# Layer 0 of a two-layer attention and FFN kernel: the order of second maxima on the vector engine, and one square root more on the scalar engine

## Chip, cores, metric

The kernel runs on one core of one Trainium2 chip. The metric is the device time of one execution in microseconds (us), as the median of several runs. Times inside an execution come from one execution taken by the hardware profiler. The engines are called PE (matrix), DVE (vector), ACT (scalar), POOL (GpSimd) and SP (the queue that issues the DMAs); each works through its own queue in order and waits for the others by semaphores.

## What is computed

Two layers over x (32 sequences of 64 tokens, width 512), all in 32-bit floats. Only layer 0 matters here: a cross attention, and an FFN in which every block of 32 hidden units keeps the one with the largest score.

```python
def _L0_xattn_ref(text, features, Wq_w, Wq_b, Wk_w, Wk_b, fn_w, qn_w, kn_w):
    features_n = rmsnorm(features, fn_w)
    Q = jnp.einsum('btd,fd->btf', text, Wq_w) + Wq_b
    K = jnp.einsum('bsd,fd->bsf', features_n, Wk_w) + Wk_b
    Q = rmsnorm(Q, qn_w)
    K = rmsnorm(K, kn_w)
    scores = jnp.einsum('btf,bsf->bts', Q, K) * scale
    attn = jax.nn.softmax(scores, axis=-1)
    return jnp.einsum('bts,bsf->btf', attn, features_n)

def _L0_ffn_ref(x, c1_w, c2_w, w1, w2t):      # INTER 1792, SPARSITY 32
    xf = x.reshape(B * T, M)
    inter = xf @ c1_w.T @ c2_w.T
    blk = inter.reshape(B * T, n_blocks, SPARSITY)
    idx = jnp.argmax(blk, axis=-1) + jnp.arange(0, INTER, SPARSITY)
    h = jax.nn.relu(jnp.einsum('bkm,bm->bk', w1[idx], xf))
    return jnp.einsum('bk,bkm->bm', h, w2t[idx]).reshape(B, T, M)

x = x + _L0_xattn_ref(_layernorm(x), ctx_4096, ...)
x = x + _L0_ffn_ref(_layernorm(x), ...)
x = x + _L1_xattn_ref(_layernorm(x), ctx_4096, ...)
x = x + _L1_ffn_ref(_layernorm(x), ...)
```

## The kernel before

The tokens lie in 16 tiles of 128, and layer 0's attention runs over them in eight groups of two tiles (`i` = 0 to 7, "pairs"). The work of neighbouring pairs is interleaved: while the keys and queries of pair `i` are made, the scores of pair `i - 1` and the values of pair `i - 2` are finished. In one round PE does, in this order: `pt` (the normed tokens turned, L181), `pk` (keys, sixteen products of 128x512, L372), `pa_t` (the softmaxed scores turned, L454), `ptk` (the keys turned), `po` (values, L466), `psc` (scores, L427), and `pq` (queries, sixteen products, L392), `ptq` (the queries turned). The other engines take the results out of PSUM. DVE adds the bias to the keys (`kb`, L375) and to the queries (`qb`, L393), scales keys by their norm (`kb`, L410), copies turned keys with a weight (`kT`, L415), and adds the values to x (L472). ACT squares rows for the norms (`scr`, L379 and L395), takes the square roots (`sq`, L354), copies `xT`, `qT` and `aT`, and takes the exponentials (`s`, L440).

The FFN's argmax for the first two pairs of tokens is computed ahead, between these steps. `PLAN` gives for (pair, place) what is put there; place 0 is ahead of the keys, 1 behind the scores, 2 behind the queries. For a group `p` of 256 tokens, `two_quarters(p, v)` makes the scores of two quarters (448 hidden units, `pi`, L277) of 128 tokens, four times per group, so that a group has eight quarters. `first_largest` finds the position of the largest score of each block of 32 in four steps: DVE takes the maximum `m` (L267) and compares (`e`, L268, which is also the last reader of the PSUM bank), POOL multiplies the comparison by a ramp that falls with the position (`e`, L272), and DVE takes the maximum again (`choice`, L273). The last step is returned as a function; `two_quarters` puts it into the list `begun`, and `choose_begun` runs whatever the list holds at the start of the next `two_quarters`, or in `turn_choice`, which turns the finished choices of a group and writes them to memory.

`pk`, `pq`, `pi` and `po` share three PSUM banks in turn (`ps_m`). So the first `pk` behind two pairs of quarters needs the bank of the fourth comparison.

POOL has other work in this stage: sums of pieces of W1 and W2 for a Strassen-Winograd scheme (`four_sums`, L127). For W2 a piece is loaded (`w2p`, one buffer), summed, stored (`w2s`), and then the next is loaded. All loads and stores stand in SP's queue, which they share with the loads of context (`ct`, `cn`) for the pair after the next.

The order on each engine is settled when the kernel is built: a list scheduler takes the instructions as they are traced, moves them by priority, and respects data, buffers and the extra edges that `tc.issue_after(ins)` adds. Such an edge puts what is traced in the block behind `ins` where both run on one engine. 

ACT holds one function table at a time; a square root behind an exponential, or the reverse, needs a load first (ACT_TABLE_LOAD). The square and the copies load none. For the last pair `queries_of` ends with an exponential of zero times `sq` into `one` (L404), behind the roots, so that the table is there when the last scores come; `scores` multiplies by `one` (L436).

Of the kernel before, what the change touches and what calls it, by code (L numbers as in the profile page):

```python
# [8 lines left out]
F32 = mybir.dt.float32  # L9
I32 = mybir.dt.int32  # L10
BF16 = mybir.dt.bfloat16
AF = mybir.ActivationFunctionType
# [4 lines left out]
P = 128  # L17
# [6 lines left out]
QW = 448  # L24
# [11 lines left out]
def tile_kernel(  # L36
# [25 lines left out]
    nc = tc.nc  # L62
# [11 lines left out]
    eps6 = const.tile([P, 1], F32, name="eps6")  # L74
# [104 lines left out]
    def transposed(ps, src):  # L179
        for c in range(C):  # L180
            nc.tensor.transpose(ps[:, c, :], src[:, c * P : (c + 1) * P], ident)  # L181


    with ExitStack() as l0:
# [74 lines left out]
        def first_largest(pi, e, choice, n):  # L259


            w, k = n * QW, n * NBQ
            mx = small.tile([P, k], F32, name=f"m{n}", tag=f"m{n}", bufs=2)
            e4 = e.rearrange("p (n a b) -> p n a b", n=n, b=BLK)
            pi = pi.rearrange("p n (a b) -> p n a b", b=BLK)
            mx3 = mx.rearrange("p (n a) -> p n a", n=n)
            nc.vector.tensor_reduce(mx3, pi, AX.X, ALU.max)  # L267
            nc.vector.tensor_tensor(  # L268
                e4, pi, mx3[:, :, :, None].to_broadcast([P, n, NBQ, BLK]), ALU.is_equal
            )  # L270
            e3 = e.rearrange("p (a b) -> p a b", b=BLK)
            nc.gpsimd.tensor_tensor(e3, e3, down[:, None, :].to_broadcast([P, k, BLK]), ALU.mult)  # L272
            return lambda: nc.vector.tensor_reduce(choice, e3, AX.X, ALU.max)  # L273

        def key_product(out, z, m, q):
            rows = slice(32 * q, 32 * q + RANK)
            nc.tensor.matmul(out, z[rows, m * P : (m + 1) * P], C2R[rows, :], start=True, stop=True)  # L277
# [10 lines left out]
        def new_choices():  # L288
            return [prepool.tile([P, 4 * NBQ], F32, name="choice", tag="choice", bufs=2) for _ in range(2)]

        with ExitStack() as pa:
            wpool = pa.enter_context(tc.tile_pool(name="l0w", bufs=1))
            wk = pa.enter_context(tc.tile_pool(name="l0work", bufs=2))
# [6 lines left out]
            bq = wpool.tile([P, D], F32, name="bq")  # L300
# [4 lines left out]
            one = wpool.tile([P, 1], F32, name="one")  # L305
# [47 lines left out]
            def norm_of(sq):  # L353
                nc.scalar.activation(sq, sq, AF.Sqrt, bias=eps6, scale=1.0 / D)  # L354
                nc.vector.reciprocal(sq, sq)
# [26 lines left out]
            def queries_of(i, xT, sq, between):  # L382

                qT = wk.tile([P, 2, C, P], F32, name=f"qT_{i}", tag="qT")
                qb = wk.tile([P, 2, D], F32, name="qb", tag="qb", bufs=1)
                last = i == NP - 1
                if last:
                    norm_of(sq[:, 2:4])
                for tt in range(2):
                    pq = ps_m.tile([P, D], F32, name="pq", tag="pm")  # L390
                    for c in range(C):
                        nc.tensor.matmul(pq, xT[:, tt, c, :], WQ[:, c, :], start=c == 0, stop=c == C - 1)  # L392
                    nc.vector.tensor_add(qb[:, tt, :], pq, bq)  # L393
                    scr = wk.tile([P, D], F32, name="scr", tag="scr", bufs=1)
                    nc.scalar.activation(scr, qb[:, tt, :], AF.Square, accum_out=sq[:, tt : tt + 1])  # L395
                between()
                for tt in range(2):
                    pt = ps_t.tile([P, C, P], F32, name="ptq", tag="pt")
                    transposed(pt, qb[:, tt, :])
                    nc.scalar.copy(qT[:, tt], pt)  # L400
                norm_of(sq[:, 0:2] if last else sq)
                if last:

                    nc.scalar.activation(one, sq[:, 0:1], AF.Exp, scale=0.0)  # L404
                return qT
# [12 lines left out]
            def scores(cn, rs, qT, sq, kT, one=None):  # L418


                psc = ps_s.tile([P, 2, S], F32, name="psc", tag="psc")
                for u in range(2):
                    for c in range(C):
                        for h in (1, 0):
                            half = slice(h * S, (h + 1) * S)
                            with tc.high_priority(offset=100) if u or c or not h else ExitStack():
                                product = nc.tensor.matmul(  # L427
                                    psc[half, u, :], qT[:, u, c, half], kT[h][:, c, u * S : (u + 1) * S],
                                    start=c == 0, stop=c == C - 1, skip_group_check=True,
                                )  # L430
                nm = small.tile([P, 2], F32, name="nm", tag="nm")
                nc.vector.tensor_reduce(nm, psc, AX.X, ALU.max, negate=True)
                if one is None:
                    most = nc.vector.tensor_mul(nm, nm, sq[:, 0:2])
                else:
                    most = nc.vector.scalar_tensor_tensor(nm, nm, one, sq[:, 0:2], ALU.mult, ALU.mult)  # L436
                s1 = wk.tile([P, 2, S], F32, name="s1", tag="s1")
                sm = small.tile([P, 2], F32, name="sm", tag="sm")
                for u in range(2):
                    nc.scalar.activation(  # L440
                        s1[:, u, :], psc[:, u, :], AF.Exp,
                        bias=nm[:, u : u + 1], scale=sq[:, u : u + 1], accum_out=sm[:, u : u + 1],
                    )

                for tt in range(2):
                    normed = nc.vector.scalar_tensor_tensor(
                        cn[:, tt, :], cn[:, tt, :], rs[:, 2 + tt : 3 + tt], fnb, ALU.mult, ALU.mult
                    )
                nc.vector.reciprocal(sm, sm)
                return s1, sm, (product.ins, most.ins, normed.ins)  # L450
# [70 lines left out]


            steps = [prep_steps(p, ps_t) for p in range(2)]
            choices, made, begun = {}, {}, []

            def step(p, k):
                made[p] = steps[p][k]()

            def choose_begun():
                while begun:  # L530
                    begun.pop(0)()

            def two_quarters(p, v):
                choose_begun()
                if v == 0:
                    choices[p] = new_choices()
                two = []
                for q in (2 * v, 2 * v + 1):
                    pi = ps_m.tile([P, 1, D], F32, name="pi0", tag="pm")[:, :, 0:QW]

                    with tc.high_priority(offset=100) if two else ExitStack():
                        key_product(pi[:, 0], made[p][1], q // 4, q % 4)
                    two.append((q, pi))
                for q, pi in two:
                    e = wk.tile([P, QW], F32, name="e0", tag="e0")
                    c = choices[p][q // 4][:, NBQ * (q % 4) : NBQ * (q % 4) + NBQ]
                    begun.append(first_largest(pi, e, c, 1))

            def turn_choice(p):
                choose_begun()  # L550
                keep_choice(p, choices[p], ps_t)
# [5 lines left out]
                (3, 2): ((step, 0, 3), (step, 1, 0)),  # L557
                (4, 0): ((step, 0, 4), (step, 1, 1)),
                (4, 1): ((two_quarters, 0, 0), (step, 1, 2)),
                (4, 2): ((two_quarters, 0, 1), (step, 1, 3)),  # L560
                (5, 0): ((two_quarters, 0, 2),),
                (5, 1): ((two_quarters, 0, 3), (step, 1, 4)),
                (5, 2): ((turn_choice, 0),),
                (6, 0): ((two_quarters, 1, 0),),
                (6, 1): ((two_quarters, 1, 1),),
                (7, 0): ((two_quarters, 1, 2),),
                (7, 1): ((choose_begun,),),
            }

# [14 lines left out]
            for i in range(NP):  # L584
# [43 lines left out]
                def between():  # L628
                    if i == NP - 1:
                        add = turn_and_add(i - 1)  # L630
                        last.append(turn_keys(kb, sq))
                        add()

                qT = queries_of(i, xT, sq, between)
                keys[i] = (rs, kb, sq, qT)
                place(i, 2)
# [7 lines left out]
            xT, choices = made[1][0], choices[1]  # L644
# [4 lines left out]
        with ExitStack() as pb:  # L649
            wk = pb.enter_context(tc.tile_pool(name="ffnwork", bufs=2, reuse_waits="tile"))  # L650
# [131 lines left out]
            for p in range(NP):  # L782
# [18 lines left out]
                if choosing:  # L801
                    choices = new_choices()
# [28 lines left out]
    with ExitStack() as pc:  # L831
# [3 lines left out]
        wk = pc.enter_context(tc.tile_pool(name="l1work", bufs=2, reuse_waits="tile"))  # L835
# [646 lines left out]
```

## Time and profile before

| | |
|---|---|
| median of 3 runs | 1842.27 us (1840.47 to 1844.25) |
| profiled execution, whole / span | 1838.82 / 1836.9 us |
| PE busy | 1811.3 us, 99% of the span |
| DVE / ACT / POOL busy | 943.2 / 654.6 / 732.1 us (51 / 36 / 40%) |
| mean granted PE clock | 0.995 |
| layer 0 attention | 0 to 184 us |
| layer 0 FFN starts (first `ph`, L720) | 184.10 us |

The span runs from the first to the last instruction; the whole execution holds 1.9 us more. PE's clock is full (1.00) but for a few stretches at half. A row of a timeline gives the start, the duration, the engine, the line and operation, what it writes and reads, the shapes, the count, and in brackets how long the engine had been idle and which instruction ended that. In the list of waits a row gives the waiting instruction, the one waited for, the sum in us, how often, and the longest. A row of stretches gives start:end, length, busy time and instructions of PE, its weight loads, DVE, ACT and POOL, then the granted clock, the share of the DMA engines and GB/s.

### The profile page before, as it was taken

The numbers are of one execution on the slowest core, as the hardware profiler recorded it, in microseconds if no ns is written. First come the engines' busy times: TensorE is split into PE (matmuls) and PEld (weight loads), VectorE is DVE, ScalarE is ACT, GpSimd is POOL, SyncE is SP. The second block draws the span as 40 slices with busy tenths as digits, with TensorE's granted clock in tenths as the row PEclk, the third lists the DMA queues.
The fourth block names the chain that finished last, engine by engine and source line by source line (L and its number), as shares of the span: only waits on it lengthen the run. The fifth ranks groups of instructions, "written<-read, shape, count | busy, mean of one in ns | idle before, by whom it ended". The sixth has DMA issues, their size and how long they took to land.

```text
span 1836.9 us, 29498 instructions
## 1 busy us (share of the span) xinstructions
PE 1811.3 (99%) x11620; PEld 1473.2 (80%) x11620; DVE 943.2 (51%) x1665; ACT 654.6 (36%) x1186; POOL 732.1 (40%) x630
## 2 busy tenths in 40 slices
PE   8999999999999999999999999999999999999998
PEld 4544988889998888888888888888888888888764
DVE  5886565555525444445444445544444554544456
ACT  4544322222113433424344334433342434434411
POOL 1442434444337676564522344324242342222412
PEclk9999999999999999999999999999999999999999
DMA  9632400000023434554444344443454434443413
GB/s 253 180 112 61 159 22 22 22 22 22 21 70 130 150 121 155 176 174 126 133 128 130 116 146 124 127 130 112 129 153 131 118 118 133 137 136 103 156 40 92
DMA packets 157210, 210.89 MB, mean 115 GB/s; under 512 B 14928, under 2 KB 95824, under 8 KB 156432
## 3 DMA queue, kind: packets, MB, share of 16 engines
q1 hardware_dynamic: 155712, 206.91, 36.7%
q10 hardware_dynamic: 1360, 2.10, 0.3%
q8 instruction: 92, 1.51, 0.3%
q14 instruction: 46, 0.38, 0.1%
HBM read 176.74 MB, written 32.21 MB: 114 GB/s over the span
## 4 chain that ended last, share of the span: by engine, by line
PE 91%; DVE 2%; ACT 2%; DMA 2%; POOL 1%; issue 1%; SPq 0%; POOLq 0%; ACTq 0%
PE b L894 52%; PE ph L720 10%; PE po L763 9%; PE sc L1058 4%; PE pv L1117 3%; PE pd L1327 2%; PE pr L1030 2%; PE pq L392 2%; PE pk L372 2%; PE pta L1099 2%; PE pt L181 1%; DMA w2p<-in_w 1%; PE ptk L1016 1%; DMA w2s<-w2p 1%; PE pi L277 1%
## 5 line engine op out<-in xcount | busy, mean ns | idle before, releaser
L1147 DVE TENSOR_TENSOR x<-x,b 128x512 f32<-128x512 f32 x224 | 153.8, 686 | 209.3 <-PE b L894 209.2
L894 PE MATMUL b<-tx,wq 128*128 128x256 f32 x1024 | 243.2, 383 | 2.1 <-POOL tx L127 1.4
L894 PE MATMUL b<-wo,so 128*128 128x256 f32 x1024 | 233.6, 381 | 3.8 <-issue 3.8
L127 POOL TENSOR_TENSOR so<-oT 128x512 f32<-128x512 f32 x64 | 81.0, 1287 | 358.5 <-ACT oT L1123 358.5
L894 PEld LDWEIGHTS b<-tx,wq 128*128 128x128 f32 x1024 | 191.0, 190 | 39.4 <-ACT keep L902 6.7
L894 PEld LDWEIGHTS b<-wo,so 128*128 128x128 f32 x1024 | 195.5, 191 | 31.1 <-issue 4.4
L894 PE MATMUL b<-xt,wq 128*128 128x256 f32 x768 | 186.2, 381 | 0.0
L894 PE MATMUL b<-wo,oT 128*128 128x256 f32 x768 | 184.9, 381 | 0.0
L1082 POOL TENSOR_TENSOR prob<-prob,mx 128x512 f32<-128x512 f32 x64 | 67.9, 1063 | 247.2 <-DVE mx L1081 129.2
L894 PEld LDWEIGHTS b<-wo,oT 128*128 128x128 f32 x768 | 145.6, 191 | 20.3 <-issue 1.0
L894 PEld LDWEIGHTS b<-xt,wq 128*128 128x128 f32 x768 | 143.1, 190 | 19.1
L1103 ACT COPY aT<-pta 128x512 f32<-128x512 f32 x64 | 34.5, 589 | 303.2 <-PE pta L1099 303.2
L902 ACT COPY keep<-b 128x512 f32<-128x512 f32 x144 | 82.2, 581 | 136.1 <-PE b L894 136.1
L894 PE MATMUL b<-wkv,sc 128*128 128x256 f32 x512 | 115.7, 379 | 0.0
L986 ACT ACTIVATE qsq<-qT 128x512 f32<-128x512 f32 x128 | 80.3, 628 | 89.1 <-DVE qT L983 88.5
L894 PEld LDWEIGHTS b<-wkv,sc 128*128 128x128 f32 x512 | 97.2, 190 | 13.2
L272 POOL TENSOR_TENSOR e<-e,down 128x896 f32<-128x896 f32 (+1 forms) x40 | 68.3, 1711 | 96.4 <-DVE e L268 90.8
L1070 DVE TENSOR_REDUCE mx<-prob 128x8 f32<-128x512 f32 x64 | 43.9, 686 | 115.6 <-POOL prob L1065 115.6
L763 PE MATMUL po<-w,gT 128*128 128x256 f32 x448 | 101.9, 382 | 0.0
L763 PEld LDWEIGHTS po<-w,gT 128*128 128x128 f32 x448 | 84.0, 190 | 18.7 <-issue 7.8
L983 DVE TENSOR_TENSOR qT<-b,keep 128x512 f32<-128x512 f32 x96 | 65.7, 687 | 58.4 <-PE b L894 58.4
L894 PE MATMUL b<-wkv,ct 128*128 128x256 f32 x384 | 94.8, 383 | 0.0
(211 smaller groups left out, 3141.6 us busy)
## 6 DMA issues: line engine op xcount, KB each, us to landing
wq<-in_wq SPq DMA_DIRECT2D x104, 256.0 KB
wo<-in_wo SPq DMA_DIRECT2D x104, 256.0 KB
wq<-wqs SPq DMA_DIRECT2D x96, 256.0 KB
wo<-wos SPq DMA_DIRECT2D x96, 256.0 KB
wkv<-in_wkv SPq DMA_DIRECT2D x52, 256.0 KB
wkv<-wks SPq DMA_DIRECT2D x48, 256.0 KB
wqs<-wq SPq DMA_DIRECT2D x32, 256.0 KB
wos<-wo SPq DMA_DIRECT2D x32, 256.0 KB
```

The lines of the kernel that those rows point to most:

```text
L127: ins = eng.tensor_tensor(s[k], *pairs[k], op)
L272: nc.gpsimd.tensor_tensor(e3, e3, down[:, None, :].to_broadcast([P, k, BLK]), ALU.mult)
L720: nc.tensor.matmul(ps[:, c, :], W1[LEFT[i]][:, d, (c0 + c) * P : (c0 + c + 1) * P], xq[RIGHT[i]][:, d, :], start=first and c == 0 and d == ...
L763: nc.tensor.matmul(ps, chunk(gq[LEFT[i]], c), W2[RIGHT[i]][:, c, :], start=first and c == 0, stop=c == HC - 1, skip_group_check=True,)
L894: last = nc.tensor.matmul(out[:, h, :], lhs(h, c), rhs(h, c), start=first and h == 0 and c == 0, stop=c == 1, skip_group_check=True,)
L902: keeps.append(nc.scalar.copy(e, ps).ins)
L983: ins = nc.vector.tensor_add(o, ps, kept.rearrange("p j (b t) -> p j b t", t=S))
L986: nc.scalar.activation(qsq[:, 4 * th : 4 * th + 4, 2 * hh : 2 * hh + 2, :], o, AF.Square)
L1058: score = nc.tensor.matmul(sc[k * S : (k + 1) * S, 4 * a + 2 * pp + b, :], qT[:, at, 2 * pp + k, :], kT[:, bb * S : (bb + 1) * S], start=T ...
L1082: ins = nc.gpsimd.tensor_tensor(pr, pr, mx[:, 1, :, None].to_broadcast([P, 8, S]), ALU.mult)
L1117: one = nc.tensor.matmul(pv[b][:, a, :], kv[rows, 2 * h + a, HD : 2 * HD], aTs[h][rows, a, :], start=True, stop=True,).ins
L1147: added.append(nc.vector.tensor_add(xq[:, i, j], xq[:, i, j], ps).ins)
```

## The change

Three things move. First, `two_quarters` calls `choose_begun(2)` at its end in place of `choose_begun()` at its start: it leaves the two youngest second maxima in the list, so that each pair of quarters' second maxima are traced behind the next pair's comparisons. Second, `choose_begun` puts each of them behind the latest `qb` (`query_added`) and the latest comparison (`compared`) traced so far. Since a comparison's result now lives longer, `e0` has four buffers in place of the pool's two. Third, for the last pair a square root of a constant is taken on ACT behind the last exponential (`exped`) of the pair before it.

```diff
@@ first_largest
-            nc.vector.tensor_tensor(
+            compared.append(nc.vector.tensor_tensor(
                 e4, pi, mx3[:, :, :, None].to_broadcast([P, n, NBQ, BLK]), ALU.is_equal
-            )
+            ).ins)
...
+        compared = []
@@ queries_of
                 if last:
                     norm_of(sq[:, 2:4])
+
+                    with tc.issue_after(exped[-1]):
+                        nc.scalar.activation(one, eps6, AF.Sqrt)
...
-                    nc.vector.tensor_add(qb[:, tt, :], pq, bq)
+                    query_added.append(nc.vector.tensor_add(qb[:, tt, :], pq, bq).ins)
@@ scores
-                    nc.scalar.activation(
+                    exped.append(nc.scalar.activation(
                         s1[:, u, :], psc[:, u, :], AF.Exp,
                         bias=nm[:, u : u + 1], scale=sq[:, u : u + 1], accum_out=sm[:, u : u + 1],
-                    )
+                    ).ins)
@@
-            choices, made, begun = {}, {}, []
+            choices, made, begun, query_added, exped = {}, {}, [], [], []
...
-            def choose_begun():
-                while begun:
-                    begun.pop(0)()
+            def choose_begun(n=0):
+
+                while len(begun) > n:
+                    with tc.issue_after(query_added[-1]), tc.issue_after(compared[-1]):
+                        begun.pop(0)()
 
             def two_quarters(p, v):
-                choose_begun()
...
                 for q, pi in two:
-                    e = wk.tile([P, QW], F32, name="e0", tag="e0")
+                    e = wk.tile([P, QW], F32, name="e0", tag="e0", bufs=4)
                     c = choices[p][q // 4][:, NBQ * (q % 4) : NBQ * (q % 4) + NBQ]
                     begun.append(first_largest(pi, e, c, 1))
+                choose_begun(2)
```

As built, DVE's order around the fourth comparison of the first group (pair 4 to 5) was `m`, `choice`, `e`, `rs`, `m`, `choice`, `e`, `m`, `kb` L410, `e`, `kb` L410, `choice`, `choice`, `kb` L375. It becomes `m`, `kb` L410, `e`, `choice`, `choice`, `rs`, `m`, `m`, `e`, `e`, `choice`, `choice`, `kb` L410, `kb` L375. Ahead of the two `qb` of pair 4 no `choice` is left. Ahead of the first `qb` of pair 5 stand quarters 4 and 5 of group 0 in place of 6 and 7, which go behind its second `qb`. Ahead of the first `qb` of pair 6 stand quarters 0 and 1 of group 1 in place of 2 and 3, which go behind its second `qb` and the next two comparisons. On ACT the last pair's order was exponentials, `scr`, `aT`, `scr`, table load, root, two `qT` copies, table load, `one`. It becomes exponentials, table load, root of the constant, `scr`, `aT`, `scr`, root, table load, `one`, two `qT` copies. On DVE the last pair's `sq` reciprocal goes ahead of the two additions to x.

## The prediction

> **What bounds the kernel now.** I read the page first: PE is busy 99% of the span, and the chain that ended last is 91% PE. A change that leaves PE's instructions alone, and this one does, can only win idle time of PE. So next come PE's waits over the first 330 us, which hold all of layer 0's attention (it ends at 184 us):
>
> ```profile
> PE pk L372 <- DVE WK L491: 5.5, 2, 5.2
> PE ptq L181 <- DVE qb L393: 2.4, 1, 2.4
> PE pk L372 <- DVE e L268: 1.2, 1, 1.2
> PE pa_t L454 <- ACT s L440: 1.1, 1, 1.1
> PE psc L427 <- DVE kT L415: 0.8, 2, 0.4
> PE psc L427 <- ACT qT L400: 0.7, 1, 0.7
> ```
>
> The first row is the start and is not touched. The others can be touched: ptq on qb, pk on e, psc on kT, and psc on qT and pa_t on s for the last pair. They are small, 6.2 us in all. What stands behind the two largest is seen in the timelines, one engine at a time. DVE:
>
> ```profile
> 105.73 0.59 DVE L267 TENSOR_REDUCE m<-pi 128x14 f32<-128x448 f32 x1
> 107.84 0.62 DVE L273 TENSOR_REDUCE choice<-e 128x14 f32<-128x448 f32 x1 [1.52 <-POOL e L272]
> 108.38 0.61 DVE L268 TENSOR_TENSOR e<-pi,m 128x448 f32<-128x448 f32 x1
> ...
> 115.43 0.74 DVE L375 SCALAR_TENSOR_TENSOR kb<-pk,rs,bk 128x512 f32<-128x512 f32 x1
> ...
> 151.13 0.62 DVE L273 TENSOR_REDUCE choice<-e 128x14 f32<-128x448 f32 x1 [3.77 <-POOL e L272]
> ```
>
> DVE stands twice in its queue at a second maximum (choice, L273) whose product POOL has not made: 1.52 us at 106.3, with the comparison e behind it that frees PE's next bank; and 3.77 us at 147.4, with both qb additions behind it. POOL is late because its products stand behind the W2 sums, which wait for a load:
>
> ```profile
> 103.81 0.73 POOL L127 TENSOR_TENSOR w2t<-w2p 128x256 f32<-128x256 f32 x1 [1.82 <-DMA w2p<-in_w]
> ...
> 147.12 0.72 POOL L127 TENSOR_TENSOR w2t<-w2p 128x256 f32<-128x256 f32 x1 [5.26 <-DMA w2p<-in_w]
> ```
>
> PE pays:
>
> ```profile
> 109.05 8.83 PE L372 MATMUL pk<-WK,ct 128*128 128x512 f32 x16 [1.17 <-DVE e L268]
> 120.32 1.15 PE L427 MATMUL psc<-kT,qT 128*64 128x64 f32 x32 [0.43 <-DVE kT L415]
> 154.15 0.66 PE L181 MATMUL ptq<-ident,qb 128*128 128x128 f32 x4 [2.36 <-DVE qb L393]
> ```
>
> The first of these pk runs 8.83 us; the next pair's sixteen take 7.03. The stretches with their granted clock (the column before the last two) tell why:
>
> ```profile
> 105.90:109.30 3.40, 2.23 (x13) 1.34 (x12) 1.88 (x5) 2.37 (x7) 2.82 (x5) 1.00 0.02 5
> 109.00:112.40 3.40, 3.35 (x5) 1.34 (x6) 2.75 (x6) 0.00 (x0) 2.00 (x2) 0.55 0.00 0
> 150.30:153.70 3.40, 1.49 (x4) 0.38 (x2) 2.10 (x5) 0.29 (x1) 1.89 (x2) 1.00 0.20 68
> 181.00:184.40 3.40, 2.79 (x10) 0.89 (x11) 2.15 (x6) 0.47 (x3) 2.22 (x2) 0.50 0.70 192
> 184.40:187.90 3.50, 3.50 (x18) 3.50 (x18) 1.86 (x3) 0.48 (x1) 0.00 (x0) 0.51 1.05 390
> ```
>
> After 1.17 us of idleness among transposes and 16-row products the clock is halved for 3.4 us (8.83 - 7.03 = 1.8 us lost). After 2.36 us behind full pq products it is not. From 181.0 it is halved for two such lengths. From 184 us on the only PE waits are five groups, 7.5 us together, none in work that the change moves.
>
> **The change, part by part.** The order of instructions on PE, POOL and SP stays the same; only DVE's and ACT's in layer 0 move. No second maximum is added or removed.
>
> *Second maxima of pair group 0 (DVE, 105.7 to 120.3).* Behind m of the fourth comparison DVE now finds kb (L410), then e, then the maxima of quarters 0 and 1, which POOL finished at 99.6. From the old end of m, in steps from the same rows (start to start when nothing waits: m, e and choice 0.53, kb 1.03 while POOL runs): kb 106.26, e 107.29 to 107.90. PE is ready at 107.88 and starts pk at 107.96, not 109.05. DVE goes on: two maxima to 108.9, rs, two m, two e to 111.1, the maxima of quarters 2 and 3 (POOL done at 107.8 and 109.6, so 2.0 us of slack) to 112.14, kb beside POOL to 112.95. L375 then starts at about 112.9, for 115.43 before. From L375 to the end of kT it was 4.83 us (115.43 to 120.26), so kT ends at 117.65 to 117.75 and psc starts at 117.72: 120.32 - 117.72 = 2.60 us earlier. PE would be ready at 116.95 (pk at 107.96, 6.9 us, then pa_t, ptk and po as before), so a wait of about 0.77 us on kT takes the place of 1.17 + 0.43; DVE stays the limit here. The halved stretch, if it goes, is won only as far as DVE allows, and is inside the 2.60. Bounds: if the clock is halved all the same, pk ends at 116.6, its second kb follows and psc starts at about 118.75, a gain of 1.6; if PE alone set it, 3.4.
>
> *Choices of the later quarters behind both qb (147 to 154).* DVE gets to qb when pq is done; ptq starts at the end of pq instead of 2.36 us later: 2.36 us, a wait that goes whole. The first maxima behind qb were finished by POOL long ago; the pair that POOL made at 150 to 152.2 is wanted about 4.9 us after ptq starts (DVE's own steps behind 154.15: m at +1.6, then e, sq, m, kb and e to +4.9). With ptq at 151.79 - 2.60 = 149.2 that is 154.1, so 1.9 us of cover even if the W2 loads do not come earlier. They should: their SP queue waits for ptk and po of PE, which move too. Without that cover the wait would stand ahead of L375, which in the trace ended 2.3 us before DVE's next wait on pk, so another 2 us would still be free. Lower bound 0 (the POOL wait comes back), upper 2.36. The 0.52 us that pt waits on qT at 133.06 stays: its chain starts at the second qb, which follows pq as before.
>
> *Four e buffers.* No instruction; with two, the first compare of the next pair would wait for the late maxima.
>
> *Square root ahead (ACT).* Before, the last pair pays here:
>
> ```profile
> 175.91 1.28 ACT L354 ACT_TABLE_LOAD   x1
> 177.20 0.29 ACT L354 ACTIVATE sq<-sq,eps 128x2 f32<-128x2 f32 x1
> 177.41 1.05 ACT L400 COPY qT<-ptq 128x512 f32<-128x512 f32 x2
> 178.47 1.28 ACT L404 ACT_TABLE_LOAD   x1
> ```
>
> The added load and root (1.28 + 0.20) fall at 171.6 to 173.1; ACT was idle for 2.10 us before its copy at 174.49, and the square put off ends at 173.9, so they are hidden; without that gap they would cost up to 1.5 on the way to aT. At the end the root runs at 175.91, but the exponential's load now stands ahead of the qT copies: load 176.2 to 177.5, one (it waits for the DVE reciprocal, about 176.4) to 177.7, copies from 177.71 instead of 177.41. So psc starts 0.30 later, at 178.32, and ends at 179.49. Then nm (0.33 for the first, by the step m to e) starts its last step at 179.87, no longer held by one until 179.97: s at 180.19 for 180.32. Gain 0.13 of the 1.28 that a removed load suggests. Bounds: 1.28 and -0.3.
>
> [...]
>
> Sum: 2.60 + 2.36 + 0.13 = 5.1 us. On the profiled execution 1838.82 (span 1836.9) that gives 1833.7. It was itself 3.45 under the median of the runs, so on the median: 1842.27 - 5.1 = **1837.2**.
>
> **Rivals.**
> *The clock takes part back.* The new wait of 0.77 us at psc lies among po, 64-column and 16-row products, the kind beside which 1.17 us sufficed at 107.9. A length of 3.4 us at half clock in the pq that follow costs 1.7: 5.1 - 1.7 = 3.4, 1838.9. Against it: 0.52 us at 133 in such a stretch did nothing. [...]
> *The wait only moves.* The maxima behind qb meet POOL late after all, ahead of kb and kT: the 2.36 comes back as a wait on kT, leaving 2.60 + 0.13 = 2.7, 1839.5. For it: the W2 load decides POOL's time at 103, 129, 138 and 147. Against: the 1.9 us and the 2 us behind it.
> *Slower: the half clock at the start of the FFN lasts on.* At 181.0 it came after the idleness around psc and pa_t, and the first 3.4 us with 2.79 us of busy PE did not lift it. Every further length costs 1.7 us of dense products. Three eat the gain; from six on (10.2 us) the kernel is slower by over 0.2%: 1842.27 - 5.1 + 10.2 = 1847.4. Against it: the first length in which PE was busy throughout ended it.
>
> **How the numbers follow.** 0.2% is 3.7 us, about what a measurement of this kernel can tell from no change (the three runs lie 3.8 apart, about two half-clock lengths). Forecast 0.70 (gain 3.8 to 7, faster); the clock 0.16 and the moved wait 0.09 (3.4 and 2.7, both within 0.2%); slower 0.05. So faster 0.70, same 0.25, slower 0.05. The range: 1833.5 is about the sum on the profiled execution, and the median's sum with both half-clock lengths at the FFN's start gone (3.4); 1841.0 is the moved wait's 1839.5 and most of one length more.
>
> **What would show it.** Right: no DVE wait on POOL ahead of e or qb between 95 and 165 us; pk of that pair at 108.0; ptq right behind pq at about 149; FFN's first ph at about 179 for 184.1; no table load behind the last second scr until the exponential's, and that ahead of qT. Wrong: psc later than 118.8, a POOL wait ahead of kT, or a first ph later than 181; or new waits of PE behind 184 us that eat what was won.

## The result, and the profile after

The kernel after takes 1834.12 us (median of 5 runs, 1833.81 to 1834.71), the kernel before 1843.47 (5 runs, 1840.47 to 1844.39): ratio 0.9959, with a 95% interval of 0.9947 to 0.9971. A second comparison (5 and 17 runs) gave 1832.50 and 1838.51, ratio 0.9967 (0.9955 to 0.9979). By these ratios the change makes the kernel faster by 0.3 to 0.4%, 6 to 7.6 us; the medians lie 9.4 us apart in the first comparison and 6.0 in the second. The forecast was 5.1 us and 1837.2. The two profiled spans, 1836.9 and 1832.3 us, differ by less than the runs; why is the main question of the experiments.

PE's waits in the first 330 us, the rows that can be set beside those of before (waiting instruction, the one waited for, sum in us, times, longest):

```profile
PE psc L432 <- DVE kT L420: 2.5, 2, 1.6
PE psc L432 <- ACT qT L405: 0.9, 1, 0.9
PE pa_t L459 <- ACT s L445: 0.7, 1, 0.7
```

The waits of pk for e and of ptq for qb are gone, and the one for kT has grown (its longest, 1.6 us, is at 53.7 us, where DVE's order is that of before; the one here is 0.9). DVE's timeline after (start, duration, engine, line and operation, and in brackets the idle time ahead):

```profile
106.55 0.59 DVE L267 TENSOR_REDUCE m<-pi 128x14 f32<-128x448 f32 x1
107.06 0.86 DVE L415 TENSOR_SCALAR kb<-kb,sq 128x512 f32<-128x512 f32 x1
107.84 0.61 DVE L268 TENSOR_TENSOR e<-pi,m 128x448 f32<-128x448 f32 x1
108.38 1.13 DVE L273 TENSOR_REDUCE choice<-e 128x14 f32<-128x448 f32 x2
...
113.67 0.74 DVE L377 SCALAR_TENSOR_TENSOR kb<-pk,rs,bk 128x512 f32<-128x512 f32 x1
...
145.51 1.12 DVE L273 TENSOR_REDUCE choice<-e 128x14 f32<-128x448 f32 x2
...
154.68 1.13 DVE L273 TENSOR_REDUCE choice<-e 128x14 f32<-128x448 f32 x2
```

No choice has a bracket any more: each finds POOL's product ready. (The critical chain of this profile puts the second choice of 108.38, at 108.92, behind a product that POOL ended at that moment. In first_only, a run with the same order here, that choice started at 107.94 and the same product of POOL ended at 108.64, so the choice doesn't need it.) And PE:

```profile
108.54 7.10 PE L374 MATMUL pk<-WK,ct 128*128 128x512 f32 x16
118.55 1.15 PE L432 MATMUL psc<-kT,qT 128*64 128x64 f32 x32 [0.91 <-DVE kT L420]
149.86 0.60 PE L181 MATMUL ptq<-ident,qb 128*128 128x128 f32 x4
```

pk starts without a wait and runs at full clock (7.10 us for 8.83); psc waits 0.91 us; ptq follows pq directly. This execution came 0.82 us later to pair 4's turns of tokens than the profile before (pt at 86.43, there 85.61), so stages are compared by their lengths. The last pair on ACT:

```profile
167.24 1.28 ACT L393 ACT_TABLE_LOAD   x1
...
171.89 1.28 ACT L409 ACT_TABLE_LOAD   x1
173.19 0.20 ACT L409 ACTIVATE one<-sq 128x1 f32<-128x1 f32 x1
173.29 1.06 ACT L405 COPY qT<-ptq 128x512 f32<-128x512 f32 x2
```

The square root's load (L393) is off the path, and the exponential's load (L409) stands ahead of the copies, as the prediction said.

For every profile the table has the lengths of three stretches of PE's timeline: from the pt of pair 4, which first_only's expectation calls that of pair 5, to the psc that waits for kT of pair 4's keys; on to the first ptq of pair 6; on to the first po of the last pair. In the profile before these points lie at 85.61, 120.32, 154.15 and 182.09 us. For filled the psc is the one behind the added products.

| kernel | pt to psc | psc to ptq | ptq to po | sum |
|---|---|---|---|---|
| before | 34.71 | 33.84 | 27.93 | 96.48 |
| before_again | 34.72 | 35.10 | 27.79 | 97.61 |
| sqrt_only | 35.14 | 35.10 | 27.66 | 97.90 |
| w2_two | 33.79 | 31.76 | 27.75 | 93.30 |
| first_only | 31.86 | 33.65 | 29.34 | 94.85 |
| second_only | 35.09 | 31.31 | 27.60 | 94.00 |
| maxima_only | 32.22 | 31.31 | 27.88 | 91.41 |
| after | 32.12 | 31.31 | 27.75 | 91.18 |
| after_again | 31.88 | 31.31 | 27.60 | 90.80 |
| exp_behind | 32.12 | 31.31 | 27.32 | 90.75 |
| cn_behind | 31.19 | 32.42 | 27.74 | 91.35 |
| best | 31.19 | 32.41 | 27.32 | 90.92 |
| best_two | 31.19 | 31.62 | 27.31 | 90.12 |
| filled | 35.38 | 38.38 | 27.73 | 101.49 |

### The profile page after: what moved, and what is told of

It is laid out like the page before. It is cut to its first block, busy times and chain, and to the rows that moved or that the text cites. A ratio compares the mean times of both kernels' runs of the same rounds, so it can differ in the third digit from the quotient of the medians.

```text
span 1832.3 us, 29495 instructions
## 1 busy us (share of the span) xinstructions
PE 1807.5 (99%) x11620; PEld 1472.1 (80%) x11620; DVE 945.5 (52%) x1665; ACT 655.2 (36%) x1187; POOL 733.7 (40%) x630
## 4 chain that ended last, share of the span: by engine, by line
PE 93%; DVE 2%; ACT 2%; POOL 1%; DMA 1%; issue 1%; SPq 0%; POOLq 0%; ACTq 0%; DVEq 0%
PE b L901 51%; PE ph L727 10%; PE po L770 9%; PE sc L1065 3%; PE pv L1124 3%; PE pq L397 3%; PE pd L1334 2%; PE pk L374 2%; PE pr L1037 2%; PE pta L1106 2%; PE pt L181 1%; PE pi L279 1%; PE ptk L1023 1%; DVE x L1413 0%; PE psc L432 0%
```

## Experiments

**before_again: the kernel before, once more, for its spread.** No edit.

> The kernel before, unchanged, to see what differs between its executions. Its five timed runs took 1840.5 to 1844.4 us, its profiled one 1838.8; the kernel after took 1833.8 to 1834.7 in all. Theory CLOCK: the waits of 1.2 and 2.4 us set off half-clock lengths of 3.4 us at some phases and not at others; then the longer executions show a lower mean granted clock, 1.7 us of time going with 3.4 us of half clock (0.0009 of the mean), and the waits of PE stay 1.2 and 2.4. Theory LOADS: the chain of W2 loads, sums and stores is longer in most executions than in the profiled one; then the mean clock is the same, and a new profile shows ptq waiting for qb for 4 to 7 us in place of 2.4, or pk for e for more than 1.2.

Measured: 1840.29 us (11 runs, 1837.85 to 1844.07), beside 30 more runs of the same kernel at 1841.17. The mean granted clock goes with the time: of the 41 executions three at 0.998 have a median of 1837.6, seventeen at 0.996 1840.2, nine at 0.995 1841.5, eight at 0.994 1841.8 and four at 0.993 1844.0 (correlation -0.78, 1.1 us for 0.001 of the mean, where 0.001 is 3.7 us of half clock: 1840 x 0.001 / 0.5). The new profile shows where. PE's timeline, then stretches with the granted clock in the third column from the right:

```profile
122.31 1.15 PE L427 MATMUL psc<-kT,qT 128*64 128x64 f32 x32 [2.10 <-DVE kT L415]
...
126.04 9.21 PE L392 MATMUL pq<-WQ,xT 128*128 128x512 f32 x16
...
157.41 0.66 PE L181 MATMUL ptq<-ident,qb 128*128 128x128 f32 x4 [0.28 <-DVE qb L393]
```

```profile
120.20:123.60 3.40, 1.30 (x37) 1.23 (x36) 3.40 (x7) 0.72 (x2) 2.08 (x1) 1.00 0.83 233
123.60:127.00 3.40, 3.40 (x8) 1.42 (x7) 2.74 (x7) 2.43 (x7) 0.05 (x1) 0.50 0.57 201
127.00:130.40 3.40, 3.40 (x6) 1.33 (x5) 2.22 (x7) 1.28 (x1) 2.17 (x2) 0.50 0.52 154
```

In this execution pk ran at full clock (7.13 us), so PE came to psc early and waited 2.10 us, and there the clock was halved for 6.8 us. The sixteen pq take 9.21 us in place of 7.03, and pi and pzs ahead of them lengthen too. The stretch psc to ptq costs 35.10 us, and the wait for qb that would have followed has shrunk to 0.28. CLOCK is borne out in the main: the clock falls with the time, though by 1.1 us for 0.001 where it wanted some 1.9, and the wait of ptq did not stay at 2.4. LOADS falls: it wanted 4 to 7 us of waiting at ptq or more than 1.2 at pk, and they were 0.28 and 1.17. The profile that the prediction rested on had its half clock at 109 us instead, in pk, where DVE set the pace anyway. The profile of sqrt_only, whose order here is that of before, shows the case of before_again again (halved from 123.1 for 6.8 us, 35.10).

**maxima_only: the change without the square root.**

```diff
-                    with tc.issue_after(exped[-1]):
-                        nc.scalar.activation(one, eps6, AF.Sqrt)
```

> The change without the square root ahead. Forecast: all but 0.1 us of the gain, so 1834.2 (within 0.5 of the kernel after). Rival: the early table is worth its 1.28 us, then 1835.4.

Measured: 1834.96 us (6 runs) beside 1841.17, ratio 0.9967 (0.9956 to 0.9978), the ratio of the whole change in its second comparison. The median lies between the forecast and the rival, and the runs can't tell these apart; the last stretch can. It is 27.88 us, for 27.75 and 27.60 with the root, so the root isn't worth 1.28 us.

**sqrt_only: the kernel before with only the square root.**

```diff
                 if last:
                     norm_of(sq[:, 2:4])
+                    with tc.issue_after(exped[-1]):
+                        nc.scalar.activation(one, eps6, AF.Sqrt)
...
```

> The kernel before with only the square root ahead. Forecast: within 0.5 us of the kernel before, because the exponential's load and the first exponential now stand ahead of the qT copies (psc some 0.3 us later, the last exponentials some 0.1 us earlier). Rival: 1.28 us faster.

Measured: 1840.11 us (12 runs) beside 1841.17, ratio 1.0001 (0.9991 to 1.0011), last stretch 27.66 us for 27.93 and 27.79. So the root is worth 0.1 to 0.3 us on the path, as forecast, and nothing that the runs can tell.

**w2_two: the kernel before, with two buffers for the loaded piece of W2.**

```diff
-                w = wpool.tile([P, 4, 256], F32, name=f"w2p_{c}", tag="w2p")
+                w = wpool.tile([P, 4, 256], F32, name=f"w2p_{c}", tag="w2p", bufs=2)
```

> The kernel before with two buffers for the loaded piece of W2, so that a load need not wait for the store of the piece before; the order on DVE stays. If POOL's lateness comes from that chain, the wait of ptq for qb goes (2.4 us or whatever it is in this execution) and the spread of the runs falls to that of the kernel after. Theory LOADS: 4 to 7 us faster than before. Theory CLOCK: 2 to 4 us faster. If the chain is not the cause: the same time.

Measured: 1838.63 us (12 runs) beside 1841.17, ratio 0.9985 (0.9976 to 0.9995): some 2.8 us faster, below the 4 to 7 of LOADS and in the 2 to 4 of CLOCK. The spread did not fall (1834.7 to 1841.4). PE's timeline:

```profile
122.07 1.15 PE L427 MATMUL psc<-kT,qT 128*64 128x64 f32 x32 [1.07 <-DVE kT L415]
...
153.82 0.60 PE L181 MATMUL ptq<-ident,qb 128*128 128x128 f32 x4
```

With the loads ahead, both waits, at pk and at ptq, go with DVE's order as it was. At ptq POOL is nearly in time: DVE waits 0.39 us for it at 149.7, in place of 3.77. At pk DVE's wait falls from 1.52 to 0.65 us, and the pt ahead of pk runs at half clock here (1.97 us for 1.09), which hides what is left. That shows the W2 chain as the cause of POOL's lateness; the change doesn't remove it, it takes DVE out from behind it. A wait of 0.57 us of ptq for qb, at 84.3, is new in this profile.

**first_only and second_only: each half of the change alone (with the root).** `choose_begun` gets a switch for its two edges, and `two_quarters` delays for one group only (0 in first_only, 1 in second_only):

```diff
             def two_quarters(p, v):
+                if p != 0:
+                    choose_begun()
...
-                choose_begun(2)
+                if p == 0:
+                    choose_begun(2, True)
```

> The change for the first group's quarters alone (and the square root); the second group's maxima run as before, ahead of the qb of pair 6. Forecast: the stretch from pt of pair 5 to psc is 2.6 us shorter than in the kernel before (32.1 for 34.7), the half clock behind psc goes, and the wait of ptq for qb at pair 6 comes back at 2 to 4 us, because the W2 chain sets POOL's time there. Net 3 to 5 us faster than before. Rival: POOL's W2 chain moves along with PE and the wait does not come back, then the whole gain of some 6 us is here.

> The change for the second group's quarters alone (and the square root). Forecast: psc of pair 4's keys as late as before (34.7 us behind pt, with the wait of 0.4 to 2.1 us for kT and the half clock behind it), and only the wait of ptq goes, which was 2.4 us in one profile of the kernel before and 0.3 to 0.8 in the others: 0.5 to 2.4 us faster than before.

Measured: first_only 1838.35 us (11 runs), ratio 0.9986 (0.9977 to 0.9994); second_only 1836.28 (6 runs), ratio 0.9970 (0.9957 to 0.9983); before beside both 1841.10. first_only wins the first stretch (31.86) and gets the wait of ptq back; PE's timeline and the stretch behind it:

```profile
151.34 0.66 PE L181 MATMUL ptq<-ident,qb 128*128 128x128 f32 x4 [1.99 <-DVE qb L398]
...
153.37 1.66 PE L181 MATMUL pt<-ident,xn 128*128 128x128 f32 x8
```

```profile
150.20:153.60 3.40, 2.26 (x15) 1.45 (x16) 2.36 (x5) 2.43 (x8) 0.00 (x0) 1.00 0.00 0
153.60:157.00 3.40, 3.40 (x11) 2.23 (x10) 3.37 (x7) 1.73 (x3) 1.77 (x2) 0.50 0.00 0
```

The wait costs 1.99 us, and the half clock behind it lengthens the last stretch by 1.6 (29.34 for 27.75). So the net is 2.6 us in the runs (1.1 to 4.2), below the 3 to 5 expected, though the interval reaches into them. second_only loses the first stretch, 35.09, as expected; this profile has its half clock in pk (8.83 us, as in the profile before) and none behind psc, and the second stretch is 31.31. In the runs it gains 5.5 us (3.1 to 7.9), more than the 0.5 to 2.4 expected. The expectation priced the wait alone. The mean clock of its six runs is 0.9973, for 0.9950 in the 22 of before beside them, which is 8.7 us of half clock less, and its profile has none at the start of the FFN, where the profile before has 6.8 us. So some half clock went too; in which places, one profile can't show. The two ratios together (0.14 and 0.30%) are about the whole change's 0.33 to 0.41%.

**filled: PE work put into the wait for kT.** The kernel before, with four products in the unused part of psc's bank; nothing reads them.

```diff
...
+                if len(added) == 4 * 4:
+                    with tc.issue_after(added[-1]):
+                        for c in range(C):
+                            nc.tensor.matmul(
+                                bank[:, 2 * S :], WQ[:, c, 0:P], WK[:, c, 0 : D - 2 * S],
+                                start=True, stop=True, skip_group_check=True,
+                            )
...
```

> The kernel before with four products more, 128x384, whose result nothing reads, ahead of the psc that waits for kT of pair 4's keys: PE work of about 1.3 us inside a wait of 0.4 to 2.1. The list scheduler also moves some DVE and ACT instructions behind it, so the total time is no clean measure; the clock is. If the wait among small products sets off the half clock there, pq behind that psc takes 7.0 us (9.2 in the profile where the clock was halved), and the mean granted clock of the runs rises from 0.9952 to about 0.997. If the half clock has another cause, the mean clock stays at 0.995.

Measured: 1844.40 us (11 runs), ratio 1.0018 (1.0009 to 1.0027). Behind the filled wait the clock stayed full: PE's timeline shows

```profile
120.97 2.85 PE L426 MATMUL psc<-WK,WQ 128*128 128x384 f32 x8
...
126.32 7.03 PE L392 MATMUL pq<-WQ,xT 128*128 128x512 f32 x16
...
150.72 1.98 PE L474 MATMUL po<-cn,aT 64*64 64x512 f32 x8 [3.07 <-ACT aT L464]
```

but the products (eight in the trace) took 2.85 us, not 1.3, and the new order on DVE and ACT made waits of 1.79 us from 144.1 and 3.07 us from 147.7, with a half clock of 6.8 us from 146.9. The mean clock of the runs is 0.9954, beside 0.9950 for before; it was to rise to 0.997, and by the expectation a mean that stays speaks for another cause. But 6.8 us of half clock is 0.0018 of the mean, as much as the filled wait was to save, so the new half clock can hide that gain. One profile with a full clock behind the filled wait agrees with CLOCK. The test is inconclusive, and what sets off the half clock stays open.

**after_again, and three attempts to get more.**

> The kernel after, unchanged, beside the variants below and more runs of the kernel before. The first comparison had a median 9.4 us apart, the two profiles 4.5. Expected from the profiles of the runs so far (the kernel before loses up to 3.3 us of pq to a half clock behind psc in two profiles of three): 5 to 8 us faster than before, 1833 to 1836.

Measured: 1832.50 us (5 runs) beside 1838.51, 6.0 us, as expected; mean clock 0.998, for 0.9953 in the 17 runs of before (the five runs of the first comparison had 0.996 to 0.997).

exp_behind puts the last pair's exponential behind the qT copies:

```diff
-                    nc.scalar.copy(qT[:, tt], pt)
+                    copied = nc.scalar.copy(qT[:, tt], pt)
                 norm_of(sq[:, 0:2] if last else sq)
                 if last:
-                    nc.scalar.activation(one, sq[:, 0:1], AF.Exp, scale=0.0)
+                    with tc.issue_after(copied.ins):
+                        nc.scalar.activation(one, sq[:, 0:1], AF.Exp, scale=0.0)
```

> The kernel after with the exponential that only loads the table put behind the qT copies of the last pair. Forecast: root at the end of the last square, copies right behind their ptq, psc about 0.9 us earlier than in the kernel after, the load under psc, the last exponentials 0.7 to 0.9 us earlier, so 0.8 us less. Rival: the load then ends later than the reductions over psc and holds the exponentials, gain under 0.3.

Measured: 1831.63 us (7 runs), ratio to before 0.9969 (0.9959 to 0.9980): not told apart from after_again. In the profile psc comes earlier (wait for qT 0.24 us), but the reductions then wait for `one`, as the rival said, on DVE:

```profile
175.24 0.22 DVE L441 SCALAR_TENSOR_TENSOR nm<-nm,one,sq 128x2 f32<-128x2 f32 x1 [0.47 <-ACT one L409]
```

The last stretch is 27.32 us, 0.3 to 0.4 less than after.

cn_behind holds the scaling of one pair's context (two instructions on DVE, 1.33 us, needed a pair later) back until the kT that PE waits for are made:

```diff
...
-                    normed = nc.vector.scalar_tensor_tensor(
+                    with tc.issue_after(turned_at[9]) if len(turned_at) == 14 else ExitStack():
+                        normed = nc.vector.scalar_tensor_tensor(
...
```

> The kernel after with the scaling of one context tile pair (two DVE instructions, 1.33 us, wanted one pair later) put behind the two kT of pair 4's keys. In the kernel after PE waits 0.9 us there for kT. If DVE is the limit of that stage, psc starts 0.9 us earlier and the time falls by 0.9; if PE is, nothing changes.

Measured: 1833.77 us (10 runs), ratio to before 0.9974 (0.9965 to 0.9984): not less than after. psc starts without a wait, and 0.9 us later the gain is gone; PE:

```profile
117.13 1.15 PE L434 MATMUL psc<-kT,qT 128*64 128x64 f32 x32
118.21 1.92 PE L279 MATMUL pi<-C2R,z 16*128 16x448 f32 x4
```

The second pi needs the bank that the first addition to x frees, and that addition now stands behind the two scalings (118.31 us). DVE was the limit; the wait only changed its place. Both edits together:

> Both edits together: 1.7 us less than the kernel after if each is worth what is forecast; at worst the same.

Measured: 1832.52 us (5 runs), ratio 0.9967 (0.9955 to 0.9979), the same as the kernel after in the runs; the profile shows the pi of 1.92 us again and the shorter last stretch of exp_behind. best_two puts the scaling behind the additions instead (`added_at[7]`, recorded in `add_values`, in place of `turned_at[9]`):

> The kernel after with the exponential's load behind the qT copies, and the scaling of the context pair put behind the additions to x (behind kT alone it made pi wait 0.9 us for a bank, which took its gain back). Forecast: psc 0.8 us earlier without the wait in pi, and 0.4 us at the end of the stage: 1.2 us less than the kernel after, some 7 less than before. If the load order of other waits takes it back: the same as the kernel after.

Measured: 1831.85 us (5 runs, 1830.33 to 1833.39) beside 1841.10, ratio 0.9948 (0.9935 to 0.9960). The profile shows neither the wait at psc nor the one in pi, but a new one of 0.37 us: the second ptq of pair 5, at 129.33, waits for its qb, and the scaling now stands ahead of that on DVE. The sum of the stretches is 90.12 us, 0.7 to 1.1 less than after, where 1.2 were expected. By its ratio it is the fastest version; it beats the kernel before beyond doubt, but the kernel after only in the profile, since the intervals overlap.

## Why the prediction was right, and what it mis-sized

*Direction and mechanism.* Both waits went, by the steps given: kb fills the time in which DVE had waited, no choice waits for POOL, qb no longer stands behind one. The median lies in the range, 0.6 us from its fast end, and the gain is clear of 0.2%. In the first comparison the gain (7.6 us by the ratio, 9.4 by the medians) is above the 3.8 to 7 that the forecast gave to it; in the second, 6.0, it is inside. No run takes out the four buffers of e or one of the two edges alone.

*2.60 for the first group.* Measured 2.59 between the two profiles (34.71 to 32.12), with a wait for kT of 0.91 us where 0.77 was forecast. maxima_only, after_again and first_only give 32.22, 31.88 and 31.86. This term held, with some luck in its parts: on the profile's own time the first kb took 0.25 us less than assumed (0.78 for 1.03), the second 0.19 more (1.00 for 0.81), and kT ended where it was said to.

*2.36 for the wait of ptq.* This is the step that was too small. Against the profile that it was taken from the stretch fell by 2.53 us (33.84 to 31.31), but against before_again by 3.79. The prediction said of the half clock: "won only as far as DVE allows, and is inside the 2.60". That holds for an execution whose half clock falls in pk at 109 us. In two of the three profiles that have the old order of maxima with W2 as it was (before, before_again, sqrt_only; filled apart), it fell behind psc, in pq, where nothing covers it. The sum of the three stretches falls by 5.3 us from the first profile to that of after (96.48 to 91.18), and by 6.4 to 6.8 from before_again to the two of after. With these the runs agree. The error was to price a stretch whose place depends on the execution from one profile of it, although the median of the runs, 3.45 us above that profile, stood in the sum.

*0.13 for the root.* 0.1 to 0.3 us between the stretches; the runs show nothing. The exponential's load took the 1.28 us that the prediction gave it: in the profile after it starts at 171.89 and `one` at 173.19, 1.30 us later; in the profile before at 178.47 and 179.77, 1.30 us as well.

*The rivals.* The clock took nothing back: none of the six profiles with the whole change (after, after_again, exp_behind, cn_behind, best, best_two) has a half clock behind that psc (in after the granted clock is 1.00 from 118.0 to 123.1). The wait did not move: the pair that the prediction gave 1.9 us of cover had its turn at 154.68 us without waiting, 3.4 us after POOL had made it. The half clock at the start of the FFN lasted two lengths of 3.4 us in one profile of after and one in the other, not longer.

*What the spans hide.* The profiles differ by only 4.6 us of span because the one of after came 0.8 us later to pair 4's pt, and lost 0.8 us at 594 us in a wait of b for keep that the profile before hasn't, against a half clock of 3.4 us instead of 6.8 at 1771 us.

## What to carry to other kernels

When a queue stalls on work that another engine makes late, moving the stalled instruction behind what is ready is worth the wait only if the engine whose time counts was waiting too, and only up to the next limit: here kT, which took back 0.9 us. Price a wait of PE together with the half clock that may follow it (here it lengthened PE's products by 1.6 to 3.3 us), and take several profiles of the unchanged kernel before the sum: where the runs lie above the profile, as here by 3.45 us, the profile is the lucky case. An edit that clears one wait should be followed to the next instruction that it delays, as the scaling of context shows, which was moved once to no avail and once to a better place, where it cost 0.37 us at the next ptq.

## What the runs showed of the hardware

In the profile before the clock stood at half from 109.35 to 112.76 us, from 181.03 to 187.86 and from 1771.64 to 1778.47, in the profile after from 176.54 to 183.37 and from 1770.56 to 1773.98 (read in stretches of 0.1 us, without the last microseconds of the span): 3.41 or 6.83 us each time. Where the half clock falls among the products differs from one execution to the next. The same wait of 1.17 us at pk was followed by half clock in before (pk 8.83 us) and by a full clock in before_again (7.13 us), which had its half clock from 123.6 on, in pq (9.21 us for 7.03).

The stretches of 3.4 us just ahead of a half clock held 2.23 us of busy PE at 105.9 in the kernel before, 1.30 at 120.2 in before_again and 2.26 at 150.2 in first_only. In w2_two the clock was halved even after a stretch in which PE had no idle time at all, but only turns and products with 16 rows or 32 columns:

```profile
105.90:109.30 3.40, 3.40 (x22) 1.46 (x20) 2.31 (x5) 3.15 (x10) 2.82 (x4) 1.00 0.01 2
109.30:112.70 3.40, 3.40 (x11) 2.44 (x11) 2.46 (x6) 1.68 (x5) 2.07 (x3) 0.51 0.00 0
```

Others left it full. In the profile before the stretch from 150.3 to 153.7 held 1.49 us of full-width pq and 1.9 us of the wait of 2.36, and the clock stayed at 1.00 to 157.1. In the kernel after PE was busy for the whole of 104.87 to 108.28 with much the same small products as in w2_two, and the clock stayed at 1.00 to 115.0. So the busy time of PE alone does not tell these stretches apart, and no run here shows what does. Nor did a busy PE always end the half clock, as the prediction read from the length at 184.4: in before_again PE was busy throughout from 123.6 to 130.4, at 0.50.

Up to 184 us ACT_TABLE_LOAD stands, besides the one at the start, 15 times in each of the two profiles, always between roots and exponentials and always 1.28 us long; squares and copies stand behind either without one.
